# Layer 3 of a four-layer kernel: each piece woven into an attention becomes eight small steps, one for each key tile

## The chip, the cores and the metric

One core of one Trainium2 chip runs the whole program as one launch. The metric is device time in microseconds from the first to the last instruction, the median of several runs. Engines are named as in the profile: PE is TensorE's matmul, PEld its weight load, DVE VectorE, ACT ScalarE, POOL GpSimd, SP SyncE.

## The reference, cut to what matters

Four layers follow each other on an activation of 2 x 128 x 64 x 64 in float32, each added to its input. Only layer 3 is touched. It normalises its input by groups and runs full softmax attention over all 4096 positions, with 8 heads of 16 channels:

```python
q = proj(wq, bq)      # y = einsum('oc,bcs->bos', w, x) + b, as (B, 8, 16, 4096)
k = proj(wk, bk)
v = proj(wv, bv)
a = jnp.einsum('bhcq,bhck->bhqk', q, k) / jnp.sqrt(jnp.float32(C))
a = jax.nn.softmax(a, axis=-1)
o = jnp.einsum('bhqk,bhck->bhcq', a, v)
...
x = x + _L3_conv_ref(_gn(x), ...)
```

The largest row maximum isn't subtracted in the softmax: the kernel computes a bound on the scores (function bound) and takes another route, a general one, if the bound is too large.

## The kernel before

The tensor X holds the activation in SBUF, 128 channels as partitions, 4096 positions for each of the two batch elements. Layer 3 treats four heads at a time (t = 0, 1), so there are four attentions, one for each (b, t). An attention (attend) runs over 8 query blocks of 512 positions (qb, NCH = 8, CH = 512), and in each over 32 key tiles of 128 positions (kt, NQT = 32).

For one key tile:

- scores (L2081 and on) makes 8 matmuls (L2089), a head in each group of 32 rows, into two PSUM tiles ps_s of 128 x 1024; the pool has three such tiles. ScalarE takes the exponential of each of the two (L2099) into weights.
- multiply (L2108) multiplies the weights of a key tile with vt, the values, and accumulates in PSUM, in a bank of the pool acc, which has two banks. It is called two key tiles late (the list waiting), so scores of tile kt stand ahead of the multiplication of tile kt - 2 in TensorE's order.
- After the last key tile, done (L2130 to L2135) copies the sums to SBUF on VectorE, divides by the denominators, adds the residual and starts the output transfers.

The next attention's inputs have to be ready when this one ends. This work is written as Python generators, and each yield ends a piece:

- bound: four VectorE reductions over q and k (L2063, one piece each), then a piece with two small VectorE operations and a matmul of one column with head_sum (L2076), the result of which goes to worst (L2078).
- folded (only once for each batch element): group statistics of X (for b = 1; the eight passes L1379, the matmuls L1385 and L1394), in one piece, and then the weights and biases with the statistics folded in (L1983 to L2002, with the matmuls L1992 and L2000), in another.
- values: 8 pieces, each of four matmuls of 96 columns (L2043) and one VectorE addition to vt (L2050).
- queries_and_keys: 8 pieces, each of one matmul of 512 columns (L2017), and then two shuffles and five more passes that make q and k (L2020 to L2033).

work() chains these. Each attention draws one piece from the chain (next(beside)) after key tiles 4, 12 and 20 of a query block. The first attention has nothing to run beside: two pieces each of keys and values are made before it, alternately, and the other 12 (early) are drawn one in every second key tile, from tile 0 of its first query block on; the chain for the next attention starts with its second block.

All of layer 3 stands under _in_order, which ties each engine to the order in which the program issues its instructions. A piece that waits on TensorE therefore holds back all later scores.

Of the kernel before, what the change touches and what calls it, by code (L numbers as in the profile page):

```python
# [18 lines left out]
CH = 512  # L19
# [1926 lines left out]
    nc.vector.tensor_scalar_mul(l3["b_qk"], l3["b_qk"], scales)  # L1946


@with_exitstack
def _layer3(ctx, tc, X, l3, cst, out, worst, here):  # L1950
    nc = tc.nc
# [19 lines left out]
    for r in residual:  # L1971
        nc.gpsimd.memset(r, 0.0)

    def folded(b, got):

        x = X[:, b, :]
        if b:
            mean, rstd = _group_stats_pow(nc, two, acc, x, cst, mhalf)
        else:
            mean, rstd = here[:, 0:1], here[:, 1:2]  # L1980
        yield
        wqk = two.tile([128, 2, 128], F32, tag="wqk", name="wqk", bufs=1)
        nc.vector.tensor_scalar_mul(  # L1983
            wqk.rearrange("p t m -> p (t m)"), w_qk.rearrange("p t j n i -> p (t j n i)"), rstd
        )
        wv = two.tile([128, 192], F32, tag="wv", name="wv", bufs=1)
        nc.vector.tensor_scalar_mul(wv, w_v, rstd)
        means = two.tile([128, 128], F32, tag="means", name="means", bufs=1)
        nc.vector.tensor_copy(means, mean.to_broadcast([128, 128]))
        ps = acc()  # L1990
        for t in range(2):
            nc.tensor.matmul(ps[:, t : t + 1], wqk[:, t, :], mean, start=True, stop=True)  # L1992
        both = two.tile([128, 2], F32, tag="both", name="both", bufs=1)
        nc.vector.tensor_sub(both, b_qk, ps[:, :2])
        bqk = two.tile([128, 3, 2], F32, tag="bqk", name="bqk", bufs=1)
        nc.vector.stream_shuffle(bqk[:, 0, :], both, OF_Q)
        nc.vector.stream_shuffle(bqk[:, 1, :], both, OF_K)
        nc.vector.tensor_scalar_mul(bqk[:, 2, :], bqk[:, 1, :], upper)
        ps = acc()
        nc.tensor.matmul(ps[:, :192], means, wv, start=True, stop=True)  # L2000
        bv = two.tile([128, 192], F32, tag="bv", name="bv", bufs=1)
        nc.vector.tensor_sub(bv, b_v, ps[:, :192])  # L2002
        got[:] = [wqk, wv, bqk, bv]
        yield

    def queries_and_keys(b, t, f, q, k, idle):

        wqk, _, bqk, _ = f
        bq, bk, bk2 = (bqk[:, n, t : t + 1] for n in range(3))
        for c in range(NCH):
            cols = slice(c * CH, (c + 1) * CH)
            ps = acc()
            nc.tensor.matmul(ps, wqk[:, t, :], X[:, b, cols], start=True, stop=True)  # L2017

            qq = two.tile([128, CH], F32, tag="qq", name="qq", bufs=1)
            nc.vector.stream_shuffle(qq, ps, OF_Q)  # L2020
            kk = two.tile([128, CH], F32, tag="kk", name="kk", bufs=1)
            nc.vector.stream_shuffle(kk, ps, OF_K)  # L2022
            hi = two.tile([128, CH], F32R, tag="hi", name="hi", bufs=1)
            if c < idle:
                nc.scalar.activation(hi, kk, AF.Identity, bias=bk)
                nc.scalar.activation(kk, kk, AF.Identity, bias=bk2, scale=upper)
                nc.scalar.activation(q[0][:, cols], qq, AF.Identity, bias=bq)
            else:
                nc.vector.tensor_scalar_add(hi, kk, bk)
                nc.vector.tensor_scalar(kk, kk, bk, upper, ALU.add, ALU.mult)  # L2030
                nc.vector.tensor_scalar_add(q[0][:, cols], qq, bq)
            nc.vector.scalar_tensor_tensor(k[:, cols], hi, sign, kk, ALU.mult, ALU.add)
            nc.vector.scalar_tensor_tensor(  # L2033
                q[1][:, cols], qq, bq, q[0][:, cols], ALU.add, ALU.subtract
            )
            yield

    def values(b, t, f, vt):
        _, wv, _, bv = f
        for kt in range(0, NQT, 4):  # L2040
            ps = acc()
            for i in range(4):
                nc.tensor.matmul(  # L2043
                    ps[:, i * 96 : (i + 1) * 96],
                    X[:, b, (kt + i) * 128 : (kt + i + 1) * 128],
                    wv[:, t * 96 : (t + 1) * 96],
                    start=True,
                    stop=True,
                )
            nc.vector.tensor_add(  # L2050
                vt[:, kt : kt + 4].rearrange("p k g a d -> p k (g a d)"),
                ps[:, :384].rearrange("p (k m) -> p k m", m=96),
                bv[:, t * 96 : (t + 1) * 96].unsqueeze(1).to_broadcast([128, 4, 96]),
            )
            yield
# [25 lines left out]
    def attend(b, t, q, k, vt, early):  # L2081
        ac = [None]

        def scores(qb, kt):
            ps = [spp.tile([128, 2, CH], F32, tag="sp", name="ps_s") for _ in range(2)]
            for n in range(2):
                for j in range(4):
                    rows = slice(32 * j, 32 * j + 32)
                    nc.tensor.matmul(  # L2089
                        ps[j // 2][:, j % 2, :],  # L2090
                        k[rows, kt * 128 : (kt + 1) * 128],
                        q[n][rows, qb * CH : (qb + 1) * CH],
                        start=(n == 0),
                        stop=(n == 1),
                    )
            w = []
            for p in range(2):
                w.append(pp.tile([128, 2, CH], F32, tag="weights", name="weights"))
                nc.scalar.activation(w[p], ps[p], AF.Exp)  # L2099
            return w  # L2100

        def multiply(qb, kt, w):
            if kt == 0:
                ac[0] = acc()
            for j in range(4):

                i = j % 2
                nc.tensor.matmul(  # L2108
                    ac[0][32 * j : 32 * j + 32, :],
                    vt[:, kt, j // 2, i : i + 2, :].rearrange("p a d -> p (a d)"),  # L2110
                    w[j // 2][:, i, :],
                    start=(kt == 0),
                    stop=(kt == NQT - 1),
                )
            if kt == NQT - 1:
                done(qb, ac[0])

        def done(qb, ps):
            cols = slice(qb * CH, (qb + 1) * CH)

            places = [
                (slice(32 * j + 16 * (j % 2), 32 * j + 16 * (j % 2) + 16),
                 slice(64 * t + 16 * j, 64 * t + 16 * j + 16))
                for j in range(4)
            ]
            xs = residual[qb % 2]
            for to, rows in places:
                nc.sync.dma_start(xs[to, :], X[rows, b, cols])
            u = two.tile([128, CH], F32, tag="u", name="u", bufs=1)
            nc.vector.tensor_copy(u, ps)  # L2130
            r = two.tile([128, CH], F32, tag="r", name="r", bufs=1)
            nc.vector.stream_shuffle(r, u, [(i + 16) % 32 for i in range(32)])  # L2132
            nc.vector.reciprocal(r, r)  # L2133
            nc.vector.tensor_mul(u, u, r)  # L2134
            nc.vector.tensor_add(u, u, xs)  # L2135
            for at, rows in places:
                nc.sync.dma_start(out[b, rows, cols], u[at, :])

        waiting = []
        for qb in range(NCH):  # L2140
            for kt in range(NQT):
                if kt % 2 == 0:
                    over = next(early, early) is early
                waiting.append((qb, kt, scores(qb, kt)))
                if len(waiting) > 2:
                    multiply(*waiting.pop(0))
                yield kt if over else None
        for x in waiting:
            multiply(*x)

    def in_turn(*gens):
        gens = list(gens)
        while gens:
            for g in list(gens):
                if next(g, gens) is gens:
                    gens.remove(g)
                else:
                    yield

    def work():  # L2160

        for b in range(B):
            f = []
            yield from folded(b, f)
            for t in range(2):
# [5 lines left out]
                keys = queries_and_keys(b, t, f, q, k, 2 * first)  # L2171
                if first:

                    for _ in range(2):
                        next(keys)
                        next(early)
                        yield
                    early = in_turn(keys, early)
                else:
                    for _ in early:  # L2180
                        yield
                    yield from keys
                yield b, t, (q, k, vt, early)
                yield from bound(b, t, q, k)

    def up_to_next(side):
        for x in side:
# [9 lines left out]
    while found:  # L2197
        b, t, got = found.pop()
        beside = up_to_next(side)
        for kt in attend(b, t, *got):  # L2200

            if kt in (4, 12, 20):
                next(beside, None)
        for _ in beside:
            pass
# [131 lines left out]
```

## Time and profile before

| | |
|---|---|
| time, median of 3 runs | 4259.99 us (4258.07 to 4268.29) |
| span of the profiled run | 4270.8 us |
| layer 3, first key tile to the end | 2307.7 to 4270.8 us |
| granted TensorE clock, mean | 0.977 |
| L2089 scores, matmul records | 8192, busy 924.6 us |
| L2108 multiplication, matmul records | 8192, busy 1093.0 us |
| L2099 exponentials | 2048, busy 1884.8 us |
| L2017 queries and keys, matmul records | 64 |
| L2043 values, matmul records | 256 |
| L2076 bound, matmul records | 8 |

A float32 matmul with full-width weights shows as two records, each with a weight load of its own; so 64 records of L2017 are 32 pieces. Busy time of overlapping instructions is counted once. Matmuls run several at a time in parts of the array, and their recorded ends are modelled: what an operation costs TensorE is read from the starts of what follows it, not from its duration. In a timeline line the columns are the start in us, the time in us, the engine, the line of the kernel, the operation, what it writes and reads, how many were merged, and in brackets the idle time before it with its releaser.

### The profile page before, as it was taken

The numbers are of one execution on the slowest core, as the hardware profiler recorded it, in microseconds if no ns is written. First come the engines' busy times: TensorE is split into PE (matmuls) and PEld (weight loads), VectorE is DVE, ScalarE is ACT, GpSimd is POOL, SyncE is SP. The second block draws the span as 40 slices with busy tenths as digits, with TensorE's granted clock in tenths as the row PEclk, the third lists the DMA queues.
The fourth block names the chain that finished last, engine by engine and source line by source line (L and its number), as shares of the span: only waits on it lengthen the run. The fifth ranks groups of instructions, "written<-read, shape, count | busy, mean of one in ns | idle before, by whom it ended". The sixth has DMA issues, their size and how long they took to land. (4 is left out here: it accounts for less than half of the span.)

```text
span 4270.8 us, 82259 instructions
## 1 busy us (share of the span) xinstructions
PE 4069.7 (95%) x35790; PEld 1563.0 (37%) x35790; DVE 2187.8 (51%) x2358; ACT 3342.3 (78%) x4051; POOL 70.7 (2%) x145
## 2 busy tenths in 40 slices
PE   6899999979999997997898999999999999999998
PEld 3522222245222223445565333333333333333332
DVE  3679999846899998986765211321132012211111
ACT  4378888734888884334654999999999999999998
POOL 1001000000000001000000000000000000000000
PEclk9999999999999999998998999999999999999999
DMA  1099960000000000003670000000000000000000
GB/s 47 2 179 187 185 102 1 1 1 2 1 1 1 1 1 10 2 2 126 246 285 4 6 4 6 6 6 4 6 6 6 4 6 6 5 5 6 6 6 4
DMA packets 158822, 158.86 MB, mean 37 GB/s; under 512 B 24809, under 2 KB 148713, under 8 KB 154354
## 3 DMA queue, kind: packets, MB, share of 16 engines
q1 hardware_dynamic: 158450, 153.50, 15.2%
q8 instruction: 282, 4.62, 0.4%
q14 instruction: 90, 0.74, 0.1%
HBM read 145.09 MB, written 73.40 MB: 51 GB/s over the span
## 5 line engine op out<-in xcount | busy, mean ns | idle before, releaser
L2099 ACT ACTIVATE weights<-ps_s 128x1024 f32<-128x1024 f32 x2048 | 1884.8, 1103 | 62.7 <-PE ps_s L2089 62.2
L1350 ACT ACTIVATE weights<-ps_s 128x1024 f32<-128x1024 f32 x1024 | 992.8, 1022 | 178.5 <-PE ps_s L1341 153.8
L2108 PE MATMUL ps_acc<-weights,vt 128*32 128x512 f32 x8192 | 1093.0, 605 | 0.0
L2089 PE MATMUL ps_s<-q,k 32*128 32x512 f32 x8192 | 924.6, 444 | 5.4 <-ACT weights L2099 5.4
L1789 DVE TENSOR_TENSOR sums<-sums,weights 128x2048 f32<-128x2048 f32 x384 | 879.2, 2289 | 44.5 <-ACT weights L1350 9.0
L2089 PEld LDWEIGHTS ps_s<-q,k 32*128 32x128 f32 x8192 | 472.7, 183 | 839.3 <-ACT weights L2099 773.6
L1341 PE MATMUL ps_s<-q,k 32*128 32x512 f32 x4096 | 649.3, 643 | 3.7 <-ACT weights L1350 1.3
L2130 DVE COPY u<-ps_acc 128x512 f32<-128x512 f32 x32 | 22.1, 692 | 1039.0 <-PE ps_acc L2108 1039.0
L1754 PE MATMUL ps_acc<-weights,vt 128*32 128x512 f32 x4096 | 550.3, 607 | 3.4 <-ACT used L1779 3.2
L1341 PEld LDWEIGHTS ps_s<-q,k 32*128 32x128 f32 x4096 | 210.5, 184 | 431.4 <-issue 212.9
L2108 PEld LDWEIGHTS ps_acc<-weights,vt 128*32 128x32 f32 x8192 | 163.2, 108 | 377.4 <-issue 365.5
L1754 PEld LDWEIGHTS ps_acc<-weights,vt 128*32 128x32 f32 x4096 | 81.1, 108 | 396.6 <-issue 378.4
L662 DVE SCALAR_TENSOR_TENSOR X<-g,w,X 128x2048 f32<-128x2048 f32 x84 | 197.4, 2351 | 2.6
L1789 DVE TENSOR_TENSOR sums<-weights 128x2048 f32<-128x2048 f32 x64 | 146.6, 2290 | 63.8 <-ACT weights L1350 63.8
L1545 PE MATMUL ps_sp<-pad,diag 32*32 32x512 f32 x4608 | 167.5, 609 | 3.0 <-DVE q L1556 2.3
L1008 PE MATMUL ps_z<-w_ri,e 128*32 128x128 f32 x2048 | 137.2, 408 | 14.6 <-DVE e L950 12.4
L2050 DVE TENSOR_TENSOR vt<-ps_acc,bv 128x384 f32<-128x384 f32 x32 | 17.8, 557 | 245.8 <-PE ps_acc L2043 245.8
L1523 PE MATMUL ps_sp<-xn,w_qkv 128*128 128x512 f32 x160 | 91.2, 709 | 33.4 <-DVE k L1556 16.0
L1545 PEld LDWEIGHTS ps_sp<-pad,diag 32*32 32x32 f32 x4608 | 96.2, 104 | 62.1 <-issue 17.1
L2020 DVE LOAD_MASK_SELECT qq<-ps_acc x32 | 0.4, 14 | 222.5 <-PE ps_acc L2017 222.5
L2133 DVE RECIPROCAL r<-r 128x512 f32<-128x512 f32 x32 | 107.3, 3353 | 1.1
L950 DVE TENSOR_SCALAR e<-ps_pe 32x136 f32<-32x136 f32 (+1 forms) x352 | 104.4, 296 | 5.0
(288 smaller groups left out, 2624.3 us busy)
## 6 DMA issues: line engine op xcount, KB each, us to landing
w_ri<-w_r SPq DMA_DIRECT2D x16, 2112.0 KB, 8.1
w_ri<-w_i SPq DMA_DIRECT2D x16, 2112.0 KB, 13.6
w_r<-in_L_conv_kr_w SPq DMA_DIRECT2D x15, 528.0 KB, 12.7
w_r<-in_L_conv_kr_x SPq DMA_DIRECT2D x15, 528.0 KB, 12.7
w_r<-in_L_conv_kr_y SPq DMA_DIRECT2D x15, 528.0 KB, 12.2
w_r<-in_L_conv_kr_z SPq DMA_DIRECT2D x15, 528.0 KB, 12.4
w_i<-in_L_conv_ki_w SPq DMA_DIRECT2D x15, 528.0 KB, 13.1
w_i<-in_L_conv_ki_x SPq DMA_DIRECT2D x15, 528.0 KB, 12.3
```

The lines of the kernel that those rows point to most:

```text
L662: nc.vector.scalar_tensor_tensor(xi, g[:, i : i + H // 2, j : j + W], w8[:, s : s + 1], xi, ALU.mult, ALU.add)
L950: nc.vector.tensor_scalar_mul(out, got[of, :, s], sign)
L1008: nc.tensor.matmul(out.rearrange("p (n f o) -> p n f o", n=2, f=2), e[:, s, 2 * j : 2 * j + 2, :].rearrange("p f x -> p (f x)"), w.rearran ...
L1341: nc.tensor.matmul(ps[j // 2][:, j % 2, :], k[rows, kt * 128 : (kt + 1) * 128], q[rows, qb * CH : (qb + 1) * CH], start=True, stop=True,)
L1350: nc.scalar.activation(w[:, 2 * p : 2 * p + 2, :], ps[p], AF.Exp)
L1545: nc.tensor.matmul(ps[r // 2][to, r % 2, :].rearrange("p (h w) -> p h w", w=W), diag[rows, grp, t, :], pad[rows, y0 : y0 + ROWS, t % 3 : t ...
L1754: nc.tensor.matmul(ac[n][rows, :], lhs(rows), w[:, j, :], start=first, stop=last)
L1789: nc.vector.tensor_add(parts[0].rearrange("p j c -> p (j c)"), t.rearrange("p j c -> p (j c)"), w.rearrange("p j c -> p (j c)"),)
L2089: nc.tensor.matmul(ps[j // 2][:, j % 2, :], k[rows, kt * 128 : (kt + 1) * 128], q[n][rows, qb * CH : (qb + 1) * CH], start=(n == 0), stop= ...
L2099: nc.scalar.activation(w[p], ps[p], AF.Exp)
L2108: nc.tensor.matmul(ac[0][32 * j : 32 * j + 32, :], vt[:, kt, j // 2, i : i + 2, :].rearrange("p a d -> p (a d)"), w[j // 2][:, i, :], star ...
L2133: nc.vector.reciprocal(r, r)
```

## The change

Each piece is cut into eight steps (PARTS = 8), and a step is drawn after each of the key tiles 2 to 25 of a query block, three pieces a block as before. The matmul of queries_and_keys becomes eight of 64 columns, one in each step. The four matmuls of a values piece come in every second step. The statistics and the fold become steps of their own, padded with empty ones to a multiple of eight; bound keeps its five steps, now one in each key tile, and is padded to eight. In the first attention four steps are drawn at each key tile, which makes a piece in two tiles as before. Before it, two pieces of keys now come ahead of two of values. The aim is that no single long insertion keeps ScalarE waiting for scores.

```diff
+PARTS = 8
...
+    def in_parts(gen):
+        n = 0
+        for _ in gen:
+            n += 1
+            yield
+        for _ in range(-n % PARTS):
+            yield
...
         x = X[:, b, :]
+        st = here
         if b:
-            mean, rstd = _group_stats_pow(nc, two, acc, x, cst, mhalf)
-        else:
-            mean, rstd = here[:, 0:1], here[:, 1:2]
-        yield
+            st = two.tile([128, 2], F32, tag="gn_got", name="gn_got")
+            yield from in_parts(_stats_steps(nc, two, acc, x, cst, mhalf, st))
+        yield from in_parts(refolded(st[:, 0:1], st[:, 1:2], got))
...
         nc.vector.tensor_copy(means, mean.to_broadcast([128, 128]))
+        yield
...
         nc.vector.tensor_scalar_mul(bqk[:, 2, :], bqk[:, 1, :], upper)
+        yield
...
-            nc.tensor.matmul(ps, wqk[:, t, :], X[:, b, cols], start=True, stop=True)
+            n = CH // PARTS
+            for i in range(PARTS):
+                part = X[:, b, c * CH + i * n : c * CH + (i + 1) * n]
+                to = ps[:, i * n : (i + 1) * n]
+                nc.tensor.matmul(to, wqk[:, t, :], part, start=True, stop=True)
+                if i < PARTS - 1:
+                    yield
...
+                for _ in range(PARTS // 4 if i < 3 else PARTS // 4 - 1):
+                    yield
...
+            over = False
             for kt in range(NQT):
-                if kt % 2 == 0:
-                    over = next(early, early) is early
+                for _ in range(PARTS // 2):
+                    if next(early, early) is early:
+                        over = over or kt == 0
+                        break
...
-                    for _ in range(2):
+                    for _ in range(2 * PARTS):
                         next(keys)
+                    for _ in range(2 * PARTS):
                         next(early)
-                        yield
                     early = in_turn(keys, early)
...
-                yield from bound(b, t, q, k)
+                yield from in_parts(bound(b, t, q, k))
...
-            if kt in (4, 12, 20):
+
+            if kt is not None and 2 <= kt < 2 + 3 * PARTS:
                 next(beside, None)
```

More of the change, by code (lines that the diff above doesn't have):

```diff
@@ L1972, in _layer3, with refolded @@
         nc.gpsimd.memset(r, 0.0)
+    def in_parts(gen):
[5 more added lines that the diff above has]
+            yield
     def folded(b, got):
         x = X[:, b, :]
+        st = here
         if b:
-            mean, rstd = _group_stats_pow(nc, two, acc, x, cst, mhalf)
-        else:
-            mean, rstd = here[:, 0:1], here[:, 1:2]
-        yield
+            st = two.tile([128, 2], F32, tag="gn_got", name="gn_got")
+            yield from in_parts(_stats_steps(nc, two, acc, x, cst, mhalf, st))
+        yield from in_parts(refolded(st[:, 0:1], st[:, 1:2], got))
+    def refolded(mean, rstd, got):
         wqk = two.tile([128, 2, 128], F32, tag="wqk", name="wqk", bufs=1)
@@ L2154, in in_turn @@
             for g in list(gens):
-                if next(g, gens) is gens:
-                    gens.remove(g)
-                else:
+                for _ in range(PARTS):
+                    if next(g, gens) is gens:
+                        gens.remove(g)
+                        break
                     yield
@@ L2172, in work @@
                 if first:
-                    for _ in range(2):
+                    for _ in range(2 * PARTS):
                         next(keys)
+                    for _ in range(2 * PARTS):
                         next(early)
-                        yield
                     early = in_turn(keys, early)
                 else:
-                    for _ in early:
-                        yield
+                    yield from early
                     yield from keys
+                    early = iter(())
                 yield b, t, (q, k, vt, early)
-                yield from bound(b, t, q, k)
+                yield from in_parts(bound(b, t, q, k))
     def up_to_next(side):
```

## The prediction

> **What bounds the kernel now.** I read the page first, then the waits, then single stretches of the timeline inside layer 3 (2298 us to the end). The page's groups show both engines at work there all the time:
>
> ```profile
> PE 4069.7 (95%) x35790; PEld 1563.0 (37%) x35790; DVE 2187.8 (51%) x2358; ACT 3342.3 (78%) x4051; POOL 70.7 (2%) x145
> L2099 ACT ACTIVATE weights<-ps_s 128x1024 f32<-128x1024 f32 x2048 | 1884.8, 1103 | 62.7 <-PE ps_s L2089 62.2
> ```
>
> 2048 exponentials in 1884.8 us are 0.92 us each, 1.84 us for the two of a key tile, and ScalarE idles only 62.7 us, nearly all of it waiting for scores. The waits of 2320 to 4250 us count these idle spells:
>
> ```profile
> ACT weights L2099 <- PE ps_s L2089: 60.2, 64, 2.4
> DVE worst L2078 <- PE ps_acc L2076: 45.9, 4, 11.5
> ```
>
> 64 spells, about one for each woven piece. One piece in the timeline (a queries-and-keys piece, then a bound's one-column matmul):
>
> ```profile
> 2764.76 1.06 PE L2108 MATMUL ps_acc<-weights,vt 128*32 128x512 f32 x8
> 2765.76 1.13 PE L2017 MATMUL ps_acc<-X,wqk 128*128 128x512 f32 x2
> 2766.82 0.74 PE L2089 MATMUL ps_s<-q,k 32*128 32x512 f32 x8
> 2767.49 1.06 PE L2108 MATMUL ps_acc<-weights,vt 128*32 128x512 f32 x8
> 2767.65 5.61 ACT L2099 ACTIVATE weights<-ps_s 128x1024 f32<-128x1024 f32 x6 [0.85 <-PE ps_s L2089]
> 2768.48 0.97 PE L2089 MATMUL ps_s<-q,k 32*128 32x512 f32 x8
> ...
> 2458.81 0.30 PEld L2076 LDWEIGHTS ps_acc<-mm,head_sum 128*128 128x128 f32 x2 [0.84 <-issue]
> 2459.13 0.30 PEld L2089 LDWEIGHTS ps_s<-q,k 32*128 32x128 f32 x8
> ```
>
> From starts: TensorE needs 2767.49 - 2766.82 = 0.67 us for scores and 2768.48 - 2767.49 = 1.00 us for the multiplication, 1.67 us a key tile when nothing holds it; the quiet period is 1.833 us, set by ScalarE. So TensorE has 0.166 us free per tile. But that slack is not stored: with three score buffers it cannot run ahead. Pieces in the chain of waits start at 2642.78 and 2658.40, 15.62 us for eight tiles, against 8 x 1.833 = 14.67: each 1.056 us piece (2765.76 to 2766.82) **costs 0.96 us**; only 0.10 us is absorbed. The one-column matmul takes 0.32 us, and the multiplication three tiles later has slipped by 0.21 us: again all but 0.10.
>
> **The Trainium skill.** TensorE: Matmul & The Clock Gate, section LDWEIGHTS, says that a weight load depends on the number of columns and not on what is streamed. The trace agrees: full-width f32 matmuls of 96 columns start 0.11 us apart, like those of 128. TensorEngine Tiling (Array Packing), Key Properties, says that changing the tiling mode drains TensorE; a one-column matmul between the 128*32 and 32*128 forms costing 0.32 us agrees. The first page, under Architectural detail, calls VectorE's queue strictly in order, and under What's actually happening it says that an idle TensorE falls to half clock. Both are visible here: no VectorE work overtakes, and the granted clock is 0.64 in 3297 to 3304 us, beside a part-idle start of an attention; ScalarE then idles 1.48 and 0.93 us more, 2.4 us together.
>
> **Part 1: small matmuls in queries_and_keys, beside an attention (24 pieces).** Each f32 matmul is two records, each with its own weight load. Size of one step of 64 columns: load 0.107, load again 0.107 (the first stream, 64/512 of 0.427 = 0.053, hides under it), second stream 0.053, drain 0.095: **0.362 us**. The same sum gives 0.31 for one column (seen 0.32) and 0.107 + 2 x 0.427 + 0.095 = 1.056 for 512 (seen 1.056). The bounds are 0.31 (streams free) and 0.42 (none hidden); I take 0.36, between two measured ends. A step in each of eight tiles makes 1.67 + 0.36 = 2.03 us a tile, over ScalarE's 1.833 by 0.195: 8 x 0.195 = 1.56 a piece against 0.96. The slack is smaller than the step's fixed cost. 24 x 0.59 = **+14 us**. Ends: +5 at 0.31, +26 at 0.42.
>
> **Part 2: values beside an attention (24 pieces).** One 96-column matmul in every second tile: 0.107 + 0.107 + 0.080 + 0.095 = 0.39 us. The next tile is empty and recovers the lead, so each loses 0.39 - 0.10: 4 x 0.29 = 1.16 against 0.96: **+5 us** (-3 to +8).
>
> **Part 3: the early pieces of the first attention (6 + 6, 2310 to 2360 us).** Four steps a tile. Today a pair of tiles with one piece takes 4.62 us (starts at 2315.47, 2324.72 and on). Four 64-column matmuls in a row are 8 loads x 0.107 + 0.053 + 0.095 = 1.00 us, so a pair becomes 2 x 2.67 = 5.34: 6 x 0.72 = +4.3. Two value matmuls a tile are about 0.62 us: 2 x 2.29 = 4.58, -0.2 in all. **+4 us.**
>
> **Part 4: before the first scores.** Both key chunks now come ahead of both value pieces, and the value addition that frees the bank for the third chunk queues on VectorE behind the second chunk's whole chain. First scores today at 2307.73. Chunk one takes 16 loads, partly at half clock: about 1.4 us later. The second chunk's shuffles then end at about 2306.5, ScalarE's three passes take 2.3, two VectorE passes and the addition 2.0, half a chunk of loads 1 to 1.7: 2312. **+4 us** (2 to 6).
>
> **Part 5: bound(), from one step in eight tiles to one in each.** This is the wait that the change adds. On VectorE, after each query block:
>
> ```profile
> 2380.12 0.69 DVE L2130 COPY u<-ps_acc 128x512 f32<-128x512 f32 x1 [21.37 <-PE ps_acc L2108]
> 2381.63 3.35 DVE L2133 RECIPROCAL r<-r 128x512 f32<-128x512 f32 x1
> 2385.80 0.69 DVE L2135 TENSOR_TENSOR u<-u,residual 128x512 f32<-128x512 f32 x1
> 2386.41 4.47 DVE L2063 TENSOR_REDUCE top<-q 128x1 f32<-128x2048 f32 x2
> 2390.80 2.28 DVE L2063 TENSOR_REDUCE top<-k 128x1 f32<-128x2048 f32 x1
> ```
>
> The done() chain takes 6.3 us from the copy; four reductions, 2.19 us apart, end 8.9 us later; the two small operations and the hand-over add 0.45: mm is ready **15.65 us** after the copy. Its matmul (L2076) is now emitted after key tile 6, not in the next block. Queued behind it on TensorE are the scores of tile 7, and ScalarE waits for those. In the first attention it comes five tiles after the copy, 5 x 1.833 = 9.2: a wait of 6.5. In the other three the copy follows the flush (2804.6), and tile 0's multiplication, issued with tile 2, ends at 2809.97; four more tiles end at 2817.3: 15.65 - 12.7 = 2.95 each. 6.5 + 3 x 2.95 = **+15 us**; the matmul itself costs 0.21 as today.
>
> **Part 6: folding batch 1.** Today its statistics matmuls and fold matmuls leave ScalarE late by 1.39 and 2.65 us (less 0.1 each, 3.85). Spread out, the statistics cost 0.45. But the fold begins at tile 2 of a block, and its L1992 at tile 3 waits for wqk behind done(): seen ready 6.7 us after the block's last multiplication (2933.71 against 2926.98), while TensorE is there after 3.67: 3.1 waited, 0.53 for its four records, 0.42 for L2000. 4.4 in all: **+0.5 us**.
>
> **Part 7: clock.** Five TensorE waits (6.5, three of 2.95, 3.1). One in three attention starts dropped the clock, for 2.4 us. I take 0.9 for the long one and 0.4 for each other: 2.5 x 2.4 = **+6 us** (0 to 12).
>
> Costed at nothing: the empty yields (no instruction), VectorE's piece work (it runs 3.7 us a chunk with nothing waiting but the next bank, which two shuffles of 0.75 free inside a tile), the extra statistics tile, and the transfers of done(). Sum: 14 + 5 + 4 + 4 + 15 + 0.5 + 6 = +48.5, on 4260: **4309 us**.
>
> **Rivals.**
> - *All hidden*: if the 0.166 us a tile held a 1.06/8 = 0.13 us step, the 64 stalls of today would vanish, -61 us, and with part 5 still there 4214. For it: ScalarE does set the quiet period. Against: 0.13 counts streaming alone, and one column costs 0.32 here. 5%, faster.
> - *Cheaper steps*: loads pulled ahead, a step at 0.25. Keys 8 x 0.083 = 0.67, -7; values 4 x 0.15 = 0.6, -9; parts 3 to 7 as above, +29: 4273. Against: no load starts before the 128*32 multiplication has drained, in any piece I looked at. 10%, around no change: of these ten I give 5 to no change, 2 to faster, 3 to slower.
> - *Clock lost for longer*: half clock after each wait for several windows, +25 to +50 on top: 4345. Only one such drop inside layer 3's attentions speaks for it. 5%.
> - My forecast: 80%, with ends from parts 1 to 7 of about +22 and +73, 4282 to 4333.
>
> The range reaches down to the cheaper steps and up to the high ends: 4272 to 4335. Faster 0.07, within 0.3% 0.05, slower 0.88.
>
> **What would show it.** L2017 becomes 512 records of 128x64; ScalarE's idle for ps_s rises from 62 us to above 90 and its spells from 64 to some 300; tiles with a key step repeat at 2.03 us, tiles with a value step slip 0.29; L2076 shows four TensorE waits on VectorE's mm, one of 6.5 and three near 3. I am wrong if key tiles repeat at 1.83, or L2076 does not wait.

## The result, and the profile after

The changed kernel takes 4313.22 us (median of 4 runs, 4308.79 to 4321.46) against 4259.03 us of the kernel before beside it: **ratio 1.0125, 95% interval 1.0104 to 1.0146**, slower by some 54 us. The forecast was 4309.

First the page's busy times, the group of the exponentials (now L2123), and three of the waits of 2320 to 4300 us (who waited for whom, us in total, times, longest):

```profile
PE 4106.7 (95%) x36238; PEld 1592.8 (37%) x36238; DVE 2188.0 (51%) x2358; ACT 3368.9 (78%) x4051; POOL 70.4 (2%) x145
...
L2123 ACT ACTIVATE weights<-ps_s 128x1024 f32<-128x1024 f32 x2048 | 1912.4, 1074 | 85.7 <-PE ps_s L2113 69.3
```

```profile
ACT weights L2123 <- PE ps_s L2113: 63.3, 141, 7.5
...
PE ps_acc L2100 <- DVE mm L2098: 11.4, 4, 6.6
...
PEld ps_acc L2007 <- DVE wqk L1997: 3.9, 1, 3.9
```

The exponentials are the same 2048, yet their busy time grew by 27.6 us (1884.8 to 1912.4) while the idle time before them grew by 23.0 (62.7 to 85.7). Overlapping instructions are counted once in busy time, so exponentials that no longer overlap look like more work, though the mean of one even fell from 1103 to 1074 ns. The two together, 50.6 us, are nearly the whole loss. L2100, bound's matmul, has its four waits; L2007, the fold's, has one.

A step of the keys' projection, in the timeline:

```profile
2720.38 1.06 PE L2132 MATMUL ps_acc<-weights,vt 128*32 128x512 f32 x8
...
2721.37 0.30 PEld L2037 LDWEIGHTS ps_acc<-X,wqk 128*128 128x128 f32 x2 [0.84 <-issue]
2721.37 0.43 PE L2037 MATMUL ps_acc<-X,wqk 128*128 128x64 f32 x2
...
2721.74 0.74 PE L2113 MATMUL ps_s<-q,k 32*128 32x512 f32 x8
...
2722.40 0.16 PEld L2132 LDWEIGHTS ps_acc<-weights,vt 128*32 128x32 f32 x8 [0.36 <-issue]
```

From 2721.37 to 2721.74 the step takes 0.37 us, and the tile repeats after 2722.40 - 2720.38 = 2.02 us, not 1.833. Its streaming, by the prediction's estimate 2 x 0.053, is less than a third of that; the rest goes to its two full-width weight loads and the change of form.

And the wait in the second block of the first attention, VectorE's lines first:

```profile
2397.63 2.27 DVE L2087 TENSOR_REDUCE top<-q 128x1 f32<-128x2048 f32 x1
2399.82 4.47 DVE L2087 TENSOR_REDUCE top<-k 128x1 f32<-128x2048 f32 x2
...
2404.52 0.22 DVE L2098 SCALAR_TENSOR_TENSOR mm<-m,lower 128x1 f32<-128x1 f32 x1
```

```profile
2404.88 0.56 PE L2100 MATMUL ps_acc<-mm,head_sum 128*128 128x1 f32 x2 [6.63 <-DVE mm L2098]
2405.37 1.23 PE L2113 MATMUL ps_s<-q,k 32*128 32x512 f32 x8
2406.53 1.94 PE L2132 MATMUL ps_acc<-weights,vt 128*32 128x512 f32 x8
```

TensorE sits idle for 6.63 us behind one column of results, and its next scores and multiplication run at half clock (1.94 us where 1.06 is usual; the granted clock was 0.50 from 2401.6 to 2408.4 us).

**Where the 52 us lie.** The start of layer 3 moved by up to 15 us between the profiled runs, with nothing changed ahead of it. So I read the stage itself: from the fold's first wqk to the start of the last exponential, 1957.8 us before and 2009.7 after, **+51.9**. Within it, a block is the time from a query block's first exponential to that of the next one, read from starts. A quiet block is 58.67 us in both kernels.

| part | before | after | difference | forecast |
|---|---|---|---|---|
| wqk to the first exponential | 12.5 | 17.2 | +4.7 | +4 |
| first block, the early pieces | 68.15 | 75.69 | +7.5 | +4 |
| keys beside, 24 pieces: block with three | 61.54 | 63.4 | 24 x 0.63 = +15 | +14 |
| values beside, 24 pieces: block with three | 61.55 | 62.15, mean of several | 24 x 0.20 = +5 | +5 |
| bound's blocks, with the clock in them | | | +17 | +15 |
| fold of batch 1, with the clock in it | | | +3 | +0.5 |
| clock, forecast apart | | | in the above | +6 |

The last rows of blocks come from what a block has beyond 58.6 (quiet) and its value pieces: bound's four blocks have 8.3, 3.1, 5.8 and 3.2 us, 20.4 together, where before had 3.6 (four matmuls at 0.2, and a clock drop of 2.8); the fold has 7.0 where it had 3.85.

### The profile page after: what moved, and what is told of

It reads as the page before. It is cut to its first block, busy times and chain, and to the rows that moved or that the text cites. A ratio compares the mean times of both kernels' runs of the same rounds, so it can differ in the third digit from the quotient of the medians.

```text
span 4319.7 us, 83180 instructions
## 1 busy us (share of the span) xinstructions
PE 4106.7 (95%) x36238; PEld 1592.8 (37%) x36238; DVE 2188.0 (51%) x2358; ACT 3368.9 (78%) x4051; POOL 70.4 (2%) x145
## 5 line engine op out<-in xcount | busy, mean ns | idle before, releaser
L2123 ACT ACTIVATE weights<-ps_s 128x1024 f32<-128x1024 f32 x2048 | 1912.4, 1074 | 85.7 <-PE ps_s L2113 69.3
L2113 PE MATMUL ps_s<-q,k 32*128 32x512 f32 x8192 | 888.1, 447 | 4.6 <-ACT weights L2123 4.6
L2113 PEld LDWEIGHTS ps_s<-q,k 32*128 32x128 f32 x8192 | 430.1, 184 | 630.5 <-ACT weights L2123 502.2
L1341 PE MATMUL ps_s<-q,k 32*128 32x512 f32 x4096 | 649.3, 643 | 3.7 <-ACT weights L1350 1.3
L1341 PEld LDWEIGHTS ps_s<-q,k 32*128 32x128 f32 x4096 | 210.5, 184 | 431.4 <-issue 212.8
L1008 PE MATMUL ps_z<-w_ri,e 128*32 128x128 f32 x2048 | 137.3, 408 | 14.5 <-DVE e L950 12.3
L2037 PEld LDWEIGHTS ps_acc<-X,wqk 128*128 128x128 f32 x512 | 76.5, 199 | 171.7 <-issue 149.9
## 6 DMA issues: line engine op xcount, KB each, us to landing
w_r<-in_L_conv_kr_w SPq DMA_DIRECT2D x15, 528.0 KB, 12.5
w_i<-in_L_conv_ki_w SPq DMA_DIRECT2D x15, 528.0 KB, 12.5
```

The lines of the kernel that those rows point to most:

```text
L1008: nc.tensor.matmul(out.rearrange("p (n f o) -> p n f o", n=2, f=2), e[:, s, 2 * j : 2 * j + 2, :].rearrange("p f x -> p (f x)"), w.rearran ...
L1341: nc.tensor.matmul(ps[j // 2][:, j % 2, :], k[rows, kt * 128 : (kt + 1) * 128], q[rows, qb * CH : (qb + 1) * CH], start=True, stop=True,)
L2037: nc.tensor.matmul(to, wqk[:, t, :], part, start=True, stop=True)
L2113: nc.tensor.matmul(ps[j // 2][:, j % 2, :], k[rows, kt * 128 : (kt + 1) * 128], q[n][rows, qb * CH : (qb + 1) * CH], start=(n == 0), stop= ...
```

## Experiments

Every kernel ran beside the kernel before, whose median was 4263.5, 4268.8 and 4270.3 us in the three groups; so ratios and blocks are what to compare. Stage and blocks are read from one profiled execution of each kernel. The last column below has four blocks of the first attention: its first, its second (bound), one with three pieces of values, one with three of keys.

| kernel | ratio to before (95%) | stage, us | first / second / values / keys block, us |
|---|---|---|---|
| before | 1 | 1957.8 | 68.15 / 58.67 / 61.55 / 61.54 |
| changed | 1.0125 (1.0104 to 1.0146) | 2009.7 | 75.69 / 69.27 / 62.21 / 63.39 |
| e1_bound_late | 1.0088 (1.007 to 1.0106) | 1995.2 | 75.59 / 59.97 / 62.16 / 63.41 |
| e2_keys_whole | 1.006 (1.0041 to 1.008) | 1982.9 | 70.46 / 69.51 / 62.12 / 61.55 |
| e3_values_whole | 1.01 (1.0083 to 1.0117) | 2004.0 | 76.44 / 69.76 / 61.55 / 63.44 |
| e4_first_as_before | 1.0092 (1.0073 to 1.0111) | 1995.8 | 69.06 / 70.05 / 62.20 / 63.44 |
| e5_columns | 0.9953 (0.9937 to 0.9968) | 1937.4 | 63.94 / 67.51 / 59.47 / 58.99 |
| e6_before_columns | 0.9963 (0.9951 to 0.9975) | 1943.8 | 67.04 / 58.67 / 60.35 / 60.93 |
| e7_before_bound_fast | 1.0038 (1.002 to 1.0055) | 1971.6 | 68.15 / 69.45 / 61.57 / 61.54 |
| e8_keys_4x128 | 1.0081 (1.0059 to 1.0103) | 1992.6 | 68.25 / 70.37 / 62.16 / 62.48 |
| e9_after_no_waits | 1.005 (1.0034 to 1.0067) | 1985.3 | 76.95 / 59.93 / 62.12 / 63.41 |
| e10_columns_no_waits | 0.9894 (0.9875 to 0.9914) | 1911.9 | 64.29 / 59.11 / 59.44 / 58.97 |

Where the clock falls, a block also differs between kernels that do the same in it: the first block of the third attention took 66.65 us in the changed kernel and 64.07 in e4. The intervals of e1, e3 and e4 overlap that of the changed kernel, so for these the blocks decide and not the time.

My theory had two causes: a fixed cost of TensorE for every inserted full-width matmul, and TensorE's waits for VectorE that come from drawing steps sooner. The rivals: all of it waits, or all of it steps and clock.

**e1_bound_late: the wait for mm.**

```diff
+        for _ in range(11):
+            yield
         m = two.tile([128, 2], F32, tag="m", name="m")
```

> The changed kernel with one thing undone in part: eleven empty steps stand between bound's four reductions and its matmul, so TensorE meets that matmul some 11 key tiles later. My theory (the wait of TensorE for VectorE's mm is about 16 us of the loss, with what the clock loses after it): 4296 us, from 4290 to 4300; the second query block of the first attention falls from 69.3 us to about 61.5, and L2100's line shows no wait for mm. Rival 1 (nearly the whole loss is this wait, the small steps being free): 4262 us. Rival 2 (the wait is hidden, since ScalarE has work queued): no change, 4313 us.

4303.7 us, above the 4290 to 4300 that I had given (the kernel before, too, was 4.4 us slower beside it than beside the changed kernel), and 14.5 us off the stage. The second block falls to 59.97, and no wait for mm is left. Both rivals fall: the wait is a part, not nothing and not everything. But I had expected 17 us. In the second attention the eleven empty steps push the statistics of batch 1 across into the next block, where they queue behind done() on VectorE. From e1's waits of 2320 to 4200 us:

```profile
PEld ps_acc L1385 <- DVE gn_mv L1382: 4.0, 1, 4.0
PE ps_acc L1385 <- DVE gn_mv L1382: 3.1, 1, 3.1
```

The wait had moved to another matmul. Like the fold's in the changed kernel, it is drawn at the beginning of a block, and what it needs from VectorE queues behind done().

**e2_keys_whole: the keys' steps.**

```diff
-            n = CH // PARTS
-            for i in range(PARTS):
-                part = X[:, b, c * CH + i * n : c * CH + (i + 1) * n]
-                to = ps[:, i * n : (i + 1) * n]
-                nc.tensor.matmul(to, wqk[:, t, :], part, start=True, stop=True)
-                if i < PARTS - 1:
-                    yield
+            for i in range(PARTS - 1):
+                yield
+            ps = acc()
+            nc.tensor.matmul(ps, wqk[:, t, :], X[:, b, cols], start=True, stop=True)
```

> The changed kernel with the keys' projection as one matmul of 512 columns in the eighth step, after seven empty ones. My theory (a step of 64 columns costs 0.36 us of TensorE whatever it streams, so eight of them cost 1.56 us against 0.96): 24 pieces give back 0.6 us each, the first attention's own 6 some 0.7 each, the start 1.5: 4293 us (4288 to 4300). A query block with three pieces of keys falls from 63.4 to 61.5 us. Rival (the small steps are no dearer than one piece, the loss is waits and clock): no change, 4313 us, block 63.4 us.

4286.8 us, ratio 1.006, a little under the 4288 to 4300 that I had given; 26.8 us off the stage where I expected 20. The keys block is back at 61.55 as forecast. The surplus is mostly at the start: the first exponential comes 11.6 us after wqk, not 17.2, even less than before the change. Two things differ there, and no run parts them: TensorE was at half clock for 2.3 of these 11.6 us, where the changed kernel had it for 14.7 of 17.2 (more on this below), and the seven empty steps put the matmul of the third piece of keys behind the first scores (2294.44 us against 2292.45), while before the change, and in part in the changed kernel, it stands ahead of them.

**e3_values_whole: the values' steps.**

```diff
+            for _ in range(PARTS - 1):
+                yield
             ps = acc()
             for i in range(4):
                 nc.tensor.matmul(ps[:, i * 96 : (i + 1) * 96], ...)
-                for _ in range(PARTS // 4 if i < 3 else PARTS // 4 - 1):
-                    yield
```

> The changed kernel with the four matmuls of a values piece together in the eighth step. My theory (0.29 us lost for each of four separate matmuls, 1.16 against 0.96 for the four at once): 24 x 0.2 = 5 us given back, 4308 us; a block with three pieces of values falls from 62.15 to 61.5 us. Rival (spreading the values does help, since each matmul fits beside the exponentials): slower than 4313, up to 4335 if all of today's 0.96 us for each were hidden by the spreading.

4307.2 us; the ratio's interval overlaps that of the changed kernel, so the time alone doesn't decide. The values block does: 61.55 against 62.15, 0.2 us a piece, and 5.7 us off the stage. Spreading the values did not help.

**e4_first_as_before: the first attention's own pieces.** Its pieces of keys, and in the same way those of values, come whole after seven empty steps, and the order ahead of it is the old one.

```diff
+            first = idle > 0
+            for _ in range(PARTS - 1 if first else 0):
+                yield
...
-                    for _ in range(2 * PARTS):
-                        next(keys)
-                    for _ in range(2 * PARTS):
-                        next(early)
+                    for _ in range(2):
+                        for _ in range(PARTS):
+                            next(keys)
+                        for _ in range(PARTS):
+                            next(early)
```

> The changed kernel with the first attention's own pieces whole, and keys and values in turn ahead of it, as before the change; all that runs beside later blocks stays in steps. My theory: the first scores come 4.7 us sooner after the fold's wqk (16.0 to 11.3 us), and the first query block falls from 75.7 to about 69 us: about 11 us, 4302 us. Rival (the half clock in the first block is chance and not the split's doing): the block falls only by the 4 us that I forecast for the split, 8 to 9 us in all with the start, or, if the order at the start did not matter, 4 us in all: 4309 us.

4300.3 us, 13.9 us off the stage where I had expected about 11. The first block, 69.06, is as expected. The start gained more, 5.9 us for 4.7 (17.2 to 11.4 us from wqk to the first exponential): as in e2, the third piece's matmul now stands behind the first scores, so the start isn't quite as before.

**e5_columns: the same steps in the multiplication's own form.** Values likewise: each matmul becomes four, 32 positions of X to the partitions from 32 * j on.

```diff
-                nc.tensor.matmul(to, wqk[:, t, :], part, start=True, stop=True)
+                for j in range(4):
+                    at = slice(32 * j, 32 * j + 32)
+                    nc.tensor.matmul(to[at, :], wqk[:, t, at], part, start=True, stop=True)
```

> The changed kernel, each small matmul of keys and values given as four matmuls of 32 output partitions, one in each column group, which is the form of the multiplication just ahead of it; the same steps, the same amount of streaming. My theory (a step's fixed cost is the two full-width weight loads and the change of form, not the streaming): a key step falls from 0.36 us to about 0.16 (2 x (0.053 + 0.027)), a value step from 0.39 to 0.21; a key piece then costs about 0.2 us against 1.56, a value piece 0.45 against 1.16: 24 x 1.36 + 24 x 0.7 = 50 us less, some 6 less in the first block: 4257 us, from 4245 to 4275, with the waits for bound still in it. A block with three pieces of keys falls from 63.4 to about 59.3 us. Rival (the fixed cost is that of any insertion, or grows with the number of instructions, now four times as many): 4313 us or more, block 63.4 or more.

4248.2 us: **faster than before**, with every step still there and bound's waits too. The timeline of the same kind of step as above:

```profile
2689.30 1.06 PE L2136 MATMUL ps_acc<-weights,vt 128*32 128x512 f32 x8
...
2690.18 0.29 PE L2039 MATMUL ps_acc<-X,wqk 128*32 128x64 f32 x8
2690.41 0.80 PE L2117 MATMUL ps_s<-q,k 32*128 32x512 f32 x8
2691.14 1.06 PE L2136 MATMUL ps_acc<-weights,vt 128*32 128x512 f32 x8
...
2691.59 0.13 PEld L2039 LDWEIGHTS ps_acc<-X,wqk 128*32 128x32 f32 x4 [0.30 <-issue]
...
2692.02 0.29 PE L2039 MATMUL ps_acc<-X,wqk 128*32 128x64 f32 x8
```

The step starts 0.88 us after the multiplication, not 1.00. There is no change of form between them, and its first four weight loads stand 0.45 us after the multiplication's start (2691.59 against 2691.14), so they run under it, where the full-width load came only after 0.99 us (2721.37 against 2720.38). The step takes 0.23 us: 0.11 more than a tile without it, inside the slack of 0.166. The tile repeats after 1.84 us. These are four times the instructions and the same streaming, at a cost of (58.99 - 58.67) / 3 = 0.11 us a keys piece where it was 1.57. So the cost was neither in the number of instructions nor in the streaming.

**e6_before_columns: the same form without steps.** Values as in e5.

```diff
-            nc.tensor.matmul(ps, wqk[:, t, :], X[:, b, cols], start=True, stop=True)
+            for j in range(4):
+                at = slice(32 * j, 32 * j + 32)
+                nc.tensor.matmul(ps[at, :], wqk[:, t, at], X[:, b, cols], start=True, stop=True)
```

> The kernel before with its pieces whole, each matmul of keys and values given as four of 32 output partitions as in the kernel before this one. My theory: a piece falls from 1.06 to about 0.88 us, as the multiplication's 0.89 of work, and costs 0.78 against 0.96: some 60 pieces x 0.18 = 10 us less than before: 4250 us; the distance between pieces eight tiles apart falls from 15.62 to 15.45 us. Rival (no fixed cost of full-width form): 4260 us, 15.62 us.

4250.7 us, ratio 0.9963. A piece of keys costs (60.93 - 58.67) / 3 = 0.75, of values 0.56. I had expected 0.78 for both.

**e7_before_bound_fast: the wait without any small step.**

```diff
-            if kt in (4, 12, 20):
+            if kt == 2 and not drawn:
+                drawn = 5
+            if kt is not None and 0 < drawn and 2 <= kt < 7:
+                drawn -= 1
+                if drawn == 0:
+                    drawn = -1
+                next(beside, None)
+            elif kt in (12, 20) or (kt == 4 and drawn < 0):
                 next(beside, None)
```

> The kernel before with one change alone: bound's five pieces are drawn at key tiles 2 to 6 of the first block that draws, and the later ones at 4, 12 and 20 as ever (so the fold of batch 1 is drawn at tile 20 and does not meet done). My theory: the wait for mm comes up without any small steps: 6.6 us in the first attention, about 2.5 in each other, up to 5 for the clock, less about 2.5 for the fold: 10 to 17 us slower, 4273 us. Rival (the waits are the small steps' doing, which delay VectorE or TensorE): 4258 us.

Ratio 1.0038, 13.8 us more in the stage (10 to 17 expected), and the second block is 69.45 us. Two of its waits, 2320 to 4200 us:

```profile
ACT weights L2099 <- PE ps_s L2089: 73.0, 71, 7.5
PE ps_acc L2076 <- DVE mm L2074: 10.1, 4, 6.7
```

The same four waits, the longest 6.7 us. They belong to the drawing of bound, not to the small matmuls.

**e8_keys_4x128: fewer, larger steps.**

```diff
-            n = CH // PARTS
-            for i in range(PARTS):
+            n = CH // 4
+            for i in range(4):
...
-                if i < PARTS - 1:
-                    yield
+                for _ in range(2 if i < 3 else 1):
+                    yield
```

> The changed kernel with a keys piece as four matmuls of 128 columns, in every second of its eight steps. My theory (cost goes by the number of insertions; a step of 128 columns is 0.107 + 0.107 + 0.107 + 0.095 = 0.42 us, of which 0.10 is absorbed): 4 x 0.32 = 1.26 us a piece, between one piece (0.96) and eight steps (1.56): 24 x 0.3 = 7 less, 4 to 6 less in the first block and at the start: 4301 us; a block with three pieces of keys falls from 63.4 to 62.5 us. Rival (cost goes by the columns streamed, or is all in the waits): no change, 4313 us, block 63.4 us.

The keys block is 62.48: (62.48 - 58.67) / 3 = 1.27 us a piece with four insertions, 1.57 with eight, 0.96 with one. The forecast was 1.26, 1.56 and 0.96.

**e9_after_no_waits and e10_columns_no_waits: the waits taken away, without and with the column form.** Here empty is 3, and 11 beside the first attention; keys and values come in turn ahead of it, as in e4.

```diff
+        for _ in range(empty):
+            yield
         m = two.tile([128, 2], F32, tag="m", name="m")
...
         nc.vector.tensor_copy(means, mean.to_broadcast([128, 128]))
-        yield
+        for _ in range(PARTS - 3):
+            yield
```

> The changed kernel with the waits for VectorE taken away by later places in the order: bound's matmul in its 8th step (its 16th beside the first attention), the fold's matmuls in steps 6 and 7 in place of 2 and 3, and keys and values in turn ahead of the first attention. The small full-width steps stay. My theory (waits and start are about 25 us of the loss, the steps' fixed cost the rest): stage from the fold's wqk to the last exponential 2009.7 - 14 - 5 - 6 = 1985 us, time 4287 us (4280 to 4295), still slower than before by some 20 us. Rival (the small steps alone gain, and only the waits spoil it): at most 4259 us.

> The same places in the order as in the kernel before this one, and keys and values as four matmuls of 32 output partitions, one in each column group. My theory (both causes removed): stage 1937.4 (with columns alone) - 14 (bound) - 5 (fold) - 2.5 (start) = 1916 us, time some 22 us below that with columns alone, 4226 us (4218 to 4236), 0.99 of before or a little less. A block with three pieces of keys stays at 58.98 us, one with values at 59.45. Rival (what the waits cost is taken back elsewhere, ScalarE or the clock): 4248 us, as with columns alone.

e9: 4293.0 us, stage 1985.3 (1985 expected). That the sum hit is in part luck: by the blocks, bound gave back some 17 us, the fold 6, the start and the first block together only 1.5, where I had put 14, 5 and 6. The time is still above before: with the waits gone, the full-width steps, and the half clock in the first block, still make it slower. e10: **4222.0 us, ratio 0.9894**, stage 1911.9 (1916 expected), the fastest of all kernels here. ScalarE's line of the waits (2320 to 4200 us) in e9, the same in e10, and e10's group of exponentials from the page:

```profile
ACT weights L2126 <- PE ps_s L2116: 39.2, 130, 2.0
```

```profile
ACT weights L2130 <- PE ps_s L2120: 9.4, 19, 1.9
```

```profile
L2130 ACT ACTIVATE weights<-ps_s 128x1024 f32<-128x1024 f32 x2048 | 1889.2, 1077 | 11.4 <-PE ps_s L2120 10.5
```

ScalarE now idles for 11.4 us where it idled for 62.7 before the change; neither kernel shows a wait for mm or wqk on TensorE. What the change was for is reached, by another form of the same matmuls and later places for what waits on VectorE.

## Why the prediction was right, and where its terms were off

**The slack is not stored (first part).** Held. Nothing in the runs let TensorE run ahead; a piece costs what its insertions cost, each less 0.10 us where the next tile is free, and less the 0.166 us of a tile where steps stand in every tile.

**Parts 1 and 2, the fixed cost.** Held almost to the digit: a step of 0.37 us against 0.362, 1.57 us a keys piece against 1.56, 1.16 a values piece against 1.16. e8 gives the third point of the law by count, and e5 shows where the fixed cost lies: with the neighbour's form and 32-column loads, half of them under the multiplication, nearly all of it is gone. The form, the width of the loads and their earlier start were not tried apart. The prediction had "no load starts before the 128*32 multiplication has drained"; that held for the full-width loads above, and e5's first loads do start before. That the next matmul starts 1.00 us after the multiplication where the form changes, and 0.88 us after it where the form stays, agrees with what the Trainium skill says in TensorEngine Tiling (Array Packing), Key Properties, on the drain at a change of mode. The 0.12 us between them hold that drain and the loads that aren't hidden, together, and no run parts them.

**Part 3, the early pieces: +7.5 for +4.** The loads were priced right: at full clock a pair of tiles with keys takes 5.40 us (forecast 5.34) and one with values 4.56 (4.58). What was missed is the clock. In the changed kernel it stayed at half until 2319.7 us, 24 us in all. Windows of 24 us from about 2.5 us after wqk, of the changed kernel and then of e8 (the columns are the window, its length, the busy times of PE, PEld, DVE, ACT and POOL, the granted clock and the DMA share with GB/s):

```profile
2296.00:2320.00 24.00, 21.46 (x108) 16.25 (x111) 11.15 (x24) 10.16 (x13) 0.00 (x0) 0.51 0.05 10
```

```profile
2297.00:2321.00 24.00, 19.48 (x132) 12.06 (x130) 12.51 (x29) 14.51 (x17) 0.00 (x0) 0.79 0.05 11
```

**Part 4, the start.** +4.7 for +4. The timeline shows the step that I had named, the third chunk's matmul waiting for the addition to vt:

```profile
2307.38 1.97 PE L2037 MATMUL ps_acc<-X,wqk 128*128 128x64 f32 x8 [1.43 <-DVE vt L2074]
```

But half clock covered 14.7 of the 17.2 us from wqk to the first exponential, and I had counted it only in part. With the steps and the old order, e9 takes 14.4 us there, 2.8 less than the changed kernel and 1.9 more than before. So the order has a share of some 2.8 us, and steps and clock together the rest; that +4 came out is in part luck.

**Part 5, bound.** The waits were 6.63 (shown above), 0.26, 2.88 and 1.60 us against 6.5 and three of 2.95:

```profile
2844.00 0.38 PE L2100 MATMUL ps_acc<-mm,head_sum 128*128 128x1 f32 x2 [0.26 <-DVE mm L2098]
...
3347.30 0.59 PE L2100 MATMUL ps_acc<-mm,head_sum 128*128 128x1 f32 x2 [2.88 <-DVE mm L2098]
...
3846.36 0.38 PE L2100 MATMUL ps_acc<-mm,head_sum 128*128 128x1 f32 x2 [1.60 <-DVE mm L2098]
```

The first and third are as worked out. At the starts of the second and fourth attention the clock fell to half while TensorE idled there (2831.7 and 3835.2 us), TensorE came later to bound's matmul, and the wait shrank by about what the clock had cost: the two terms are not independent, and I had added them. With the clock the part is +17 against 15 + some of 6. The waits alone were 11.4 us, 4 us under the forecast; that the total fits is in part luck, since the clock lost more here and in the first block than forecast.

**Part 6, the fold.** TensorE's wait was as forecast (PEld's 3.9 us holds the usual 0.84, so 3.1). Half clock from 2899.9 us, inside that wait, to 2906.8 is the likely rest of the +3; no run has so long a wait there without a fall of the clock.

**Part 7.** In three of the five waits the clock fell, where I had counted 2.5, and at two of three attention starts where before it was one.

**A sign that I read wrong beforehand:** I said ScalarE's idle time for scores would pass 90 us in some 300 spells. For scores it was 69.3 us by the group, 63.3 in 141 spells by the waits. Small slips of 0.2 us show as less overlap between exponentials, in busy time and not in idle time.

The rivals: that all would be hidden failed in the form tried, and e5 shows under which form it nearly holds. Cheaper steps were not seen with full-width matmuls. A longer loss of clock was seen in the first block alone, not beside the later ones.

## What to carry to other kernels

Before cutting a long insertion into small ones, price one small one from the starts around the smallest that is already there, here a one-column matmul of 0.32 us; and compare all the steps, each less the free time of one period, with the cost of the whole (here 8 x 0.196 = 1.57 us against 0.96). Try inserted matmuls in the tile form of their neighbour; here small steps then fitted. And when pieces are drawn sooner, look on every engine they touch for what stands ahead of them there: a matmul of one column held TensorE for 6.6 us because VectorE was still busy with a finished block.

## What the runs showed that I had not expected

**A busy TensorE that stays at half clock.** In four kernels (the changed one, e1, e3, e9) the clock stays at half for 23.9 us from some 2.4 us after wqk, in e9 with TensorE busy throughout by its records:

```profile
2294.50:2318.50 24.00, 24.00 (x119) 17.32 (x118) 11.14 (x24) 12.05 (x14) 0.00 (x0) 0.50 0.05 11
```

Those four have full-width matmuls of 64 columns in the first block. The other kernels (keys whole, in 128 columns, or in column form) spend 6.8 to 13.6 us of that stretch at half clock. Recorded busy time was not enough to bring the clock up; what it follows instead was not tried, so the cause stays open.

**Wander of the earlier layers.** The fold's wqk came at 2281.6 to 2296.5 us in the profiled runs though nothing ahead of it was changed, as much as several of the effects here; the blocks repeat to about 0.1 us where the clock does not fall.
